# Attention copies pinned in program order, layer 3's stages in forward order, and one layer-3 block less ahead of the second attention table

## The chip, the cores and the metric

The kernel runs on one core of one Trainium2 chip. The metric is the device time of one execution in microseconds (us). A profiled execution also has a span, from its first to its last instruction; all times of day in this document ("at 2089.8 us") count from the start of that span. The engines are TensorE (PE: matrix products; its weight loads are listed apart as PEld), VectorE (DVE), ScalarE (ACT), GpSimd (POOL) and SyncE (SP, which here only issues DMAs).

## The reference

x has 128 graphs of 64 nodes with 256 features, all in float32; adj is one 64x64 matrix. Four layers follow one another, each as `x = layernorm(x + layer(x))`. The change lies in the last two:

```
# layer 2: attention along 512 edges (src, dst), 4 heads of 64
Xq, Xv = H @ W_lin.T, H @ W_val.T
e    = a . leaky_relu(Xq[:, src] + Xq[:, dst], 0.2) + log(A0[src, dst] + 1e-8)
attn = softmax of e over the edges with one src
Y    = sum over those edges of attn * Xv[:, dst];   return Y @ W_out.T

# layer 3: a filter in the eigenbasis U of adj's normalized Laplacian
agg = U.T applied to the nodes of x
h   = relu(agg @ W1 + b1)
return U applied to the nodes of (h @ W2 + b2)
```

Layer 0 (two graph convolutions and four small LSTMs) and layer 1 (a graph convolution with two batch norms) come first and take most of the time; the change does not touch them.

## The kernel before, in words

X stays on the chip as 64 tiles of 128x256 (two graphs each). Layer 2 works on **pairs** of tiles, numbered 0 to 31, in two **halves** of 16 pairs. Layer 3 works on **blocks** of four tiles, numbered 0 to 15.

*Scoring* (`scores`, from L1914) makes the edge scores of a pair. `maps` (L1901) multiplies the transposed X by both weight matrices (L1907); ACT copies the results out as xq (L1909) and xv (L1910), and SP stores xv in DRAM. PE then expands xq to edges (l, L1930), ACT copies l to xs (L1937), DVE applies the leaky relu (L1938), and PE reduces to scores (sc, L1884).

*Softmax* (`softmax`, from L1952) normalizes the scores of one half and scatters the weights to DRAM by eight indirect DMAs that POOL issues (L2002). `fetch(half)` (L2007) reads them back as **table** M2, eight DMAs of 512 KB, four issued by SP and four by POOL (L2012). Table one is the first half's, table two the second half's.

*Values* (`values`, L2040) has one step for each pair k. `load(k+1)` copies eight columns of the table on ACT (mc, L2019, two buffers) and has POOL load that pair's xv from DRAM (xr, L2022, three buffers). `mixed(k)` multiplies the two on PE (L2034, sixteen 64x64 products into two PSUM tiles, of which there are two), and ACT copies each to yT (L2037). PE multiplies the yT of the pair before by W_out (the output product, L2055). `Norm.add` (L1228) adds that to X on DVE (L1234) and takes statistics (L1237, L1238). After four tiles `Norm.flush` (L1243) computes the scale in a chain of small instructions (is_t L1212 on DVE, is_s L1214 on ACT, is_r L1215 to L1217, ln_rs L1218 and ln_sh L1249 on DVE), and ACT normalizes the four tiles (L1253).

*Layer 3* has four stages for a block q. `basis(q)` (L2115) applies U to X on PE (L2120), ACT copies the result (ag, L2122), and POOL adds a constant row to the four tiles of X (L2124). `first_map(q)` (L2126) multiplies by W1 (L2130), and DVE adds the bias and cuts at zero (h, L2133). `back(q)` (L2135) applies U again (L2138), copied by ACT (uh, L2140). `second_map(q)` (L2142) multiplies by W2 (L2148), adds to X on DVE and normalizes as above, and SP writes the tiles out (L2154). `blocks` (L2156) is a generator: its step q runs second_map(q-3), back(q-2), first_map(q-1) and basis(q).

Each of these parts is a generator, and `run(...)` names the order in which their next steps are emitted: this is the **program order**. A scheduler then orders the instructions of each engine by its own planned times and may move an instruction ahead of others on its engine. `tc.keep_in_program_order` takes that freedom from an instruction. On the chip each engine runs its list strictly in order and waits on semaphores.

The order around the change is: scoring steps beside softmax steps of half 0; `fetch(0)`; scoring beside the first seven value steps; then softmax of half 1 beside value steps, with the first layer-3 blocks; `fetch(1)`; a few value steps and blocks; eight turns of two value steps and one block; two value steps; and the remaining blocks.

Of the kernel before, what the change touches and what calls it, by code (L numbers as in the profile page):

```python
# [1259 lines left out]
def tile_adj_resnorm(ctx: ExitStack, tc: tile.TileContext, I: dict, out: bass.AP, layers: int = 4):  # L1260
    nc = tc.nc
    v, s, te = nc.vector, nc.scalar, nc.tensor
# [3 lines left out]
    def load(name, shape, src, eng=nc.sync, dtype=F32):  # L1266
        t = const.tile(shape, dtype, tag=name, name=name)
        eng.dma_start(t, src)
        return t
# [17 lines left out]
    xt = I["x"].rearrange("(t b) n d -> (b n) t d", b=2)  # L1287
    nc.sync.dma_start(X[:, :4, :], xt[:, :4, :])
    ident = load("ident", [P, P], I["ident"], s)
    adj = load("adj", [N, N], I["adj"], s)  # L1290
    wg1 = lh.tile([P, 2, D], F32, tag="wg1", name="wg1")
    nc.sync.dma_start(wg1, kio(I["Wg1"]))
# [4 lines left out]
    s.dma_start(bl, I["bih"])  # L1297
    s.dma_start(bh, I["bhh"])
    cst = load("cst", [N, CONST_COLS], I["consts"], nc.gpsimd)

    ones = const.tile([P, P], F32, tag="ones", name="ones")
# [182 lines left out]
    with tc.tile_pool(name="lw", bufs=1) as lw, tc.tile_pool(  # L1484
# [141 lines left out]
        def residual(g, H, pool, tag):  # L1626
            hj = H.rearrange("p c (m j) -> p c j m", j=TG)
            for j in range(0, TG, 2):
                ps = pool.tile([P, 512], F32, tag=tag, name=tag)
                for i in range(2):  # L1630
                    for c in range(2):
                        te.transpose(ps[:, i * D + c * P : i * D + (c + 1) * P], hj[:, c, j + i, :], ident)
                ln.add(g * TG + j, ps, 2)
                yield
# [21 lines left out]
        with tc.tile_pool(name="l0g", bufs=1) as l0:  # L1656
            back = iter(())
            for g in range(NT // TG):
# [18 lines left out]
                if g < NT // TG - 1:  # L1677
                    back = residual(g, last, pr, "pr")
# [58 lines left out]
    back = residual(NT // TG - 1, H, pp, "ps")  # L1737
# [23 lines left out]
    for q in range(NQ):  # L1761
        h = sm.tile([P, 4, 512], F32, tag="h", name="h")
# [70 lines left out]
    with ExitStack() as l2:  # L1833
# [27 lines left out]
        sc, M2 = [None, None], [None, None]  # L1861
# [145 lines left out]
        def fetch(half):  # L2007

            M2[half] = lw.tile([P, N, P], F32, tag="M2", name="M2")
            for n0 in range(0, N, 16):  # L2010
                for b in range(2):
                    (nc.sync, nc.gpsimd)[b].dma_start(  # L2012
                        M2[half][b * N : (b + 1) * N, n0 : n0 + 16, :],
                        attn_d[b][: N * N, :].rearrange("(d n) q -> d n q", n=N)[:, n0 : n0 + 16, :])

        def load(k):
            half, u_ = divmod(k, HU)
            m = sm.tile([P, 2, 2, 2, N], F32, tag="mc", name="mc")
            s.copy(m.rearrange("p c i h n -> p (c i h) n"),  # L2019
                   M2[half][:, :, u_ * 8 : u_ * 8 + 8].rearrange("p n q -> p q n"))  # L2020
            x = sm.tile([P, 2, D], F32, tag="xr", name="xr", bufs=3)
            nc.gpsimd.dma_start(x, xvd[k])  # L2022
            return m, x
# [16 lines left out]
        def values():  # L2040

            K = NT // 2
            now, yT = load(0), None
            for k in range(K + 1):
                y = yT
                if k < K:
                    m, x = now
                    if k < K - 1:
                        now = load(k + 1)
                    yT = mixed(m, x)  # L2050
                if k:
                    po = scratch()
                    for i in range(2):
                        for c in range(2):
                            te.matmul(po[:, i * D : (i + 1) * D], y[:, i, c, :], wo[:, c, :], start=(c == 0), stop=(c == 1))  # L2055
                    ln.add(2 * (k - 1), po, 2)
                yield

        def run(*steps):
            for x in steps:  # L2060
                next(x, None)
# [11 lines left out]
        val = values()  # L2073
# [34 lines left out]
        with tc.tile_pool(name="l3s", bufs=2) as s3, tc.tile_pool(name="l3p", bufs=6, space=PSUM) as p3:  # L2108
            bank = lambda: p3.tile([P, 512], F32, tag="ps", name="ps")
            ln3 = Norm(nc, s3, X, 4, act=True)  # L2110
            ov = out.rearrange("(t b) n d -> (b n) t d", b=2)
            four = lambda a: a.rearrange("p (j n) -> p j n", j=4)
            ag, h, uh = {}, {}, {}

            def basis(q):  # L2115
                ag[q] = s3.tile([P, 2, 512], F32, tag="ag", name="ag")
                for k in range(2):
                    ps = bank()
                    for j in range(4):
                        te.matmul(ps[:, j * P : (j + 1) * P], X[:, q * 4 + j, k * P : (k + 1) * P], bdu,  # L2120
                                  start=True, stop=True)
                    s.copy(ag[q][:, k, :], ps)  # L2122
                for j in range(4):
                    nc.gpsimd.tensor_tensor(X[:, q * 4 + j, :], X[:, q * 4 + j, :], cb, ALU.add)  # L2124

            def first_map(q):  # L2126
                ps, a = bank(), ag.pop(q)
                for j in range(4):
                    for k in range(2):
                        te.matmul(ps[:, j * P : (j + 1) * P], a[:, k, j * P : (j + 1) * P], w1[:, k, :],  # L2130
                                  start=(k == 0), stop=(k == 1))
                h[q] = s3.tile([P, 4, P], F32, tag="h3", name="h3")
                v.tensor_tensor(h[q], four(ps), nb1[:, None, :].to_broadcast([P, 4, P]), ALU.max)  # L2133

            def back(q):  # L2135
                ps, a = bank(), h.pop(q)
                for j in range(4):
                    te.matmul(ps[:, j * P : (j + 1) * P], a[:, j, :], bdut, start=True, stop=True)  # L2138
                uh[q] = s3.tile([P, 4, P], F32, tag="uh", name="uh")
                s.copy(uh[q], four(ps))  # L2140

            def second_map(q):  # L2142
                a = uh.pop(q)
                n = 4 if q < NT // 4 - 1 else 2
                for j in range(0, 4, 2):
                    ps = bank()
                    for i in range(2):
                        te.matmul(ps[:, i * D : (i + 1) * D], a[:, j + i, :], w2, start=True, stop=True)  # L2148
                    ln3.add(q * 4 + j, ps, 2)
                    t = q * 4 + j + 2  # L2150
                    if t % n == 0:
                        if n == 2:
                            ln3.flush()
                        nc.sync.dma_start(ov[:, t - n : t, :], X[:, t - n : t, :])  # L2154

            def blocks():  # L2156

                NQ = NT // 4
                for q in range(NQ + 3):
                    for k, stage in ((3, second_map), (2, back), (1, first_map), (0, basis)):  # L2160
                        if 0 <= q - k < NQ:
                            stage(q - k)
                    yield

            l3 = blocks()
            sf = soft[1]
            run(sf, val, sf, val, sf, val, sf, val, sf, l3, l3, val, l3, val)
            fetch(1)
            run(l3, val, l3, val, l3)
            run(*[val, val, l3] * 8, val, val, *[l3] * (NT // 4))  # L2170
        valuing.close()

# [61 lines left out]
```

## Time and profile before

| | us |
|---|---|
| median of three runs (2421.91 to 2425.59) | 2422.01 |
| the profiled execution | 2417.21 |
| its span | 2415.4 |
| PE busy in the span | 2292.2 (95%) |
| DVE busy | 1798.8 (74%) |
| ACT busy | 969.7 (40%) |
| POOL busy | 86.3 (4%) |
| span from 2113 to 2192 (scoring beside values): PE busy | 75.60 of 79.00 |
| span from 2196 to 2269 (around table two): PE busy | 65.23 of 73.00 |
| one later turn (2326.88 to 2340.86): PE busy | 12.24 of 13.98 |
| the same turn: DVE, ACT, POOL busy | 8.78, 8.90, 3.83 |
| end (2382.16 to 2415.40): PE, DVE busy | 22.16, 24.40 of 33.24 |

A row of a timeline holds the start in us, the duration in us, the engine, the line of the kernel, the operation, what it writes and reads, and how many instructions were merged; in brackets stands the time that the engine was idle ahead of it and the instruction that released it. A float32 product is two passes on PE, so sixteen products of the program are 32 in the trace. In the list of waits the three numbers are the total in us, the number of waits and the longest. The clock row and the "PEclk" figures give the clock that was granted to PE as a share of its full speed.

### The profile page before, as it was taken

The numbers are of one execution on the slowest core, as the hardware profiler recorded it, in microseconds if no ns is written. First come the engines' busy times: TensorE is split into PE (matmuls) and PEld (weight loads), VectorE is DVE, ScalarE is ACT, GpSimd is POOL, SyncE is SP. The second block draws the span as 40 slices with busy tenths as digits, with TensorE's granted clock in tenths as the row PEclk, the third lists the DMA queues.
The fourth block names the chain that finished last, engine by engine and source line by source line (L and its number), as shares of the span: only waits on it lengthen the run. The fifth ranks groups of instructions, "written<-read, shape, count | busy, mean of one in ns | idle before, by whom it ended". The sixth has DMA issues, their size and how long they took to land. (4 is left out here: it accounts for less than half of the span.)

```text
span 2415.4 us, 29678 instructions
## 1 busy us (share of the span) xinstructions
PE 2292.2 (95%) x9084; PEld 1233.0 (51%) x9084; DVE 1798.8 (74%) x8355; ACT 969.7 (40%) x1751; POOL 86.3 (4%) x131
## 2 busy tenths in 40 slices
PE   7999999999999999999999999998979999899887
PEld 5544654444565544665444644554434433346776
DVE  4666766677887888888888898787958876456656
ACT  2323322242333243332343322334438865456565
POOL 0000000000000000000000000000000000103321
PEclk9999999999999999999999999999989999899999
DMA  6000000000100010100001000012210100311521
GB/s 217 20 18 36 1 35 1 25 28 18 53 1 35 3 51 18 53 35 1 35 36 45 8 18 18 18 51 96 79 36 27 40 30 27 97 39 47 138 80 66
DMA packets 44645, 101.52 MB, mean 42 GB/s; under 512 B 5280, under 2 KB 23840, under 8 KB 43200
## 3 DMA queue, kind: packets, MB, share of 16 engines
q1 hardware_dynamic: 38640, 84.90, 10.1%
q0 software_dynamic: 3984, 14.40, 2.1%
q8 instruction: 72, 1.18, 0.2%
q14 instruction: 93, 0.76, 0.1%
q10 hardware_dynamic: 1856, 0.28, 0.1%
HBM read 67.97 MB, written 31.59 MB: 41 GB/s over the span
## 5 line engine op out<-in xcount | busy, mean ns | idle before, releaser
L1595 PE MATMUL pq<-H,wi 128*128 128x512 f32 (+1 forms) x2016 | 835.0, 546 | 6.1 <-DVE H L1624 4.0
L1601 ACT ACTIVATE gate<-pq,bl 128x512 f32<-128x512 f32 (+1 forms) x504 | 317.2, 634 | 790.0 <-PE pq L1599 645.6
L1595 PEld LDWEIGHTS pq<-H,wi 128*128 128x128 f32 x2016 | 371.7, 190 | 330.6 <-issue 255.4
L1599 PE MATMUL pq<-lh,wh 128*128 128x512 f32 (+1 forms) x1152 | 482.7, 535 | 16.2 <-DVE lh L1619 12.9
L1599 PEld LDWEIGHTS pq<-lh,wh 128*128 128x128 f32 x1152 | 212.8, 190 | 213.2 <-issue 128.3
L1938 DVE SCALAR_TENSOR_TENSOR xs<-xs 128x512 f32<-128x512 f32 x256 | 165.5, 682 | 65.9 <-ACT xs L1937 64.9
L1937 ACT COPY xs<-l 128x512 f32<-128x512 f32 x256 | 136.5, 586 | 74.6 <-PE l L1930 42.2
L1617 ACT ACTIVATE gate<-lc 128x512 f32<-128x512 f32 (+1 forms) x144 | 83.5, 580 | 166.2 <-DVE lc L1613 79.9
L1930 PE MATMUL l<-edge_s,xq 64*128 64x512 f32 x512 | 134.7, 623 | 7.5 <-ACT xs L1937 3.9
L1907 PE MATMUL m<-wqv,xT 128*128 128x512 f32 x256 | 121.9, 614 | 0.8 <-DVE xT L1898 0.8
L1769 PE MATMUL ps<-h,w 128*128 128x512 f32 x256 | 113.4, 602 | 6.9 <-ACT h L1764 6.9
L1750 PE MATMUL ps<-at,w 128*128 128x512 f32 x256 | 115.0, 600 | 3.8 <-ACT at L1746 3.2
L1253 ACT ACTIVATE X<-X,ln_sh,ln_rs 128x256 f32<-128x256 f32 x192 | 99.5, 590 | 34.2 <-DVE ln_sh L1249 33.8
L1237 DVE BATCH_NORM_STATS2 ln_st<-X 128x6 f32<-128x256 f32 x256 | 98.4, 416 | 2.3
L142 DVE COPY AQR<-eps 64x192 f32<-64x192 f32 (+1 forms) x125 | 35.0, 280 | 81.3 <-PE eps L148 81.1
L2022 POOL DMA_DIRECT2D xr<-xv x32 | 17.5, 548 | 2051.0 <-ACT y L1784 1889.5
L1907 PEld LDWEIGHTS m<-wqv,xT 128*128 128x128 f32 x256 | 46.0, 192 | 75.1 <-issue 59.2
L1769 PEld LDWEIGHTS ps<-h,w 128*128 128x128 f32 x256 | 48.6, 192 | 66.5 <-issue 56.5
L1234 DVE TENSOR_TENSOR X<-ps,X 128x512 f32<-128x512 f32 x66 | 44.6, 675 | 46.4 <-PE ps L2055 44.1
L1615 DVE TENSOR_TENSOR gate<-gate 128x512 f32<-128x512 f32 (+1 forms) x72 | 43.4, 604 | 46.0 <-ACT gate L1601 45.5
L1750 PEld LDWEIGHTS ps<-at,w 128*128 128x128 f32 x256 | 46.6, 189 | 58.7 <-issue 46.1
L1930 PEld LDWEIGHTS l<-edge_s,xq 64*128 64x128 f32 x512 | 46.3, 188 | 58.0 <-issue 32.1
(573 smaller groups left out, 3281.9 us busy)
## 6 DMA issues: line engine op xcount, KB each, us to landing
wi<-in_WihT_dram SPq DMA_DIRECT2D x16, 1024.0 KB, 4.9
wh<-in_WhhT_dram SPq DMA_DIRECT2D x12, 1024.0 KB, 6.9
X<-in_x_dram SPq DMA_DIRECT2D x16, 512.0 KB, 8.9
xd<-X SPq DMA_DIRECT2D x16, 512.0 KB, 2.7
X<-xd SPq DMA_DIRECT2D x16, 512.0 KB, 3.4
xv<-xv SPq DMA_DIRECT2D x32, 256.0 KB, 2.0
xr<-xv POOLq DMA_DIRECT2D x32, 256.0 KB, 2.9
out_dram<-X SPq DMA_DIRECT2D x15, 512.0 KB, 2.9
```

What stands on the lines that cost most here:

```text
L1237: nc.vector.bn_stats(st, self.X[:, k, :])
L1253: nc.scalar.activation(x, x, AF.Identity, bias=sh[:, k : k + 1], scale=rs[:, k : k + 1])
L1595: te.matmul(ps, wi[:, kk, o * P : (o + 1) * P], at(kk, k), start=(kk == 0), stop=(k == 0 and kk == 1))
L1599: te.matmul(ps, wh[:, kk, o * P : (o + 1) * P], hst[:, kk, :M], start=False, stop=(kk == 1))
L1601: s.activation(gates[gt][:, c, :M], ps, AF.Tanh if gt == 2 else AF.Sigmoid, bias=bl[:, p - 1, o : o + 1])
L1617: s.activation(g[2], cs, AF.Tanh)
L1750: te.matmul(ps, w1[:, k, c * P : (c + 1) * P], at[:, k, :], start=(k == 0), stop=(k == 1))
L1769: te.matmul(ps, w2[:, k, c * P : (c + 1) * P], h[:, k, :], start=(k == 0), stop=(k == 3))
L1907: te.matmul(ps, xT[:, i, c, :], wqv[:, c, :], start=(c == 0), stop=(c == 1))
L1930: mms.append(te.matmul(pl[i][:, b, :], xq[i][r, c * P : (c + 1) * P], GG[r, :], start=True, stop=True))
L1937: taken.append(s.copy(x, pl[i][:, b, :]))
L1938: ready.append(v.scalar_tensor_tensor(x, x, 0.2, x, ALU.mult, ALU.max))
```

## The change

Three edits, all in the last two layers.

1. In `load`, the copy mc of the first two pairs of each half (u_ below 2: pairs 0, 1, 16 and 17) is kept in program order.
2. A step of `blocks` runs its stages as basis(q), first_map(q-1), back(q-2), second_map(q-3), the reverse of the order before.
3. Ahead of the eight turns, `run` emits two blocks after `fetch(1)` instead of three; the block left out is emitted at the end.

```diff
         def load(k):
             half, u_ = divmod(k, HU)
             m = sm.tile([P, 2, 2, 2, N], F32, tag="mc", name="mc")
-            s.copy(m.rearrange("p c i h n -> p (c i h) n"),
-                   M2[half][:, :, u_ * 8 : u_ * 8 + 8].rearrange("p n q -> p q n"))
+            c = s.copy(m.rearrange("p c i h n -> p (c i h) n"),
+                       M2[half][:, :, u_ * 8 : u_ * 8 + 8].rearrange("p n q -> p q n"))
+            if u_ < 2:
+                tc.keep_in_program_order(c)
...
                 for q in range(NQ + 3):
-                    for k, stage in ((3, second_map), (2, back), (1, first_map), (0, basis)):
+                    for k, stage in enumerate((basis, first_map, back, second_map)):
                         if 0 <= q - k < NQ:
                             stage(q - k)
                     yield
...
             run(sf, val, sf, val, sf, val, sf, val, sf, l3, l3, val, l3, val)
             fetch(1)
-            run(l3, val, l3, val, l3)
+            run(l3, val, l3, val)
             run(*[val, val, l3] * 8, val, val, *[l3] * (NT // 4))
```

No arithmetic changes, and no instruction is added or left out. Behind the edit the lines of the kernel move by two (L2034 becomes L2036, and so on from `load` down).

## The prediction

> **What bounds the kernel now.** The page comes first: TensorE (PE) is busy almost everywhere and dips only in the last sixth.
>
> ```profile
> PE   7999999999999999999999999998979999899887
> PEclk9999999999999999999999999999989999899999
> ```
>
> The change touches nothing before 2076 us, so the rest is read from 1900 us on: first the waits there.
>
> ```profile
> ACT mc L2019 <- DMA M<-attn_d: 13.5, 1, 13.5
> PE m L1896 <- ACT xv L1910: 10.4, 1, 10.4
> PE m L2034 <- ACT yT L2037: 17.7, 10, 3.5
> ```
>
> Three stalls carry the argument. ScalarE (ACT) waits 13.5 us for the first attention table, and PE sits 10.4 us behind it. Then PE waits ten times for yT. The timelines of ACT (two lines) and PE at the first stall:
>
> ```profile
> 2075.25 1.07 ACT L1937 COPY xs<-l 128x512 f32<-128x512 f32 x2 [0.75 <-PE sc L1884]
> 2089.78 2.01 ACT L2019 COPY mc<-M 128x512 f32<-128x512 f32 x2 [13.46 <-DMA M<-attn_d]
> ...
> 2079.99 1.98 PE L1907 MATMUL m<-wqv,xT 128*128 128x512 f32 x4
> 2092.38 1.12 PE L1896 MATMUL m<-ident,X 128*128 128x128 f32 x4 [10.41 <-ACT xv L1910]
> 2094.60 3.79 PE L1930 MATMUL l<-edge_s,xq 64*128 64x512 f32 x8 [1.10 <-ACT xq L1909]
> 2098.32 1.35 PE L1884 MATMUL sc<-xs,az 128*32 128x512 f32 x8
> ```
>
> L1930 x8 takes 3.79 us after the gap and 1.99 us elsewhere: PE comes back at half clock. One turn of the later loop (two value steps, one layer-3 block) lasts 13.97 us, of which PE works 12.23. PE first, then ACT, VectorE (DVE) and GpSimd (POOL):
>
> ```profile
> 2289.56 0.98 PE L2034 MATMUL m<-mc,xr 64*64 64x64 f32 x32
> 2290.47 1.99 PE L2055 MATMUL ps<-wo,yT 128*128 128x256 f32 x8
> 2292.39 0.68 PE L2034 MATMUL m<-mc,xr 64*64 64x64 f32 x16
> 2294.81 0.68 PE L2034 MATMUL m<-mc,xr 64*64 64x64 f32 x16 [1.74 <-ACT yT L2037]
> ...
> 2290.40 1.04 ACT L2122 COPY ag<-ps 128x512 f32<-128x512 f32 x2
> 2291.35 0.37 ACT L2037 COPY yT<-m 128x256 f32<-128x256 f32 x1
> 2292.43 2.08 ACT L1253 ACTIVATE X<-X,ln_sh,ln_rs 128x256 f32<-128x256 f32 x4 [0.71 <-DVE ln_sh L1249]
> 2294.41 0.35 ACT L2037 COPY yT<-m 128x256 f32<-128x256 f32 x1
> ...
> 2290.74 0.49 DVE L1216 TENSOR_TENSOR is_r<-is_r,is_t 128x4 f32<-128x4 f32 x1
> 2291.27 0.65 DVE L1217 SCALAR_TENSOR_TENSOR is_r<-is_r,is_s 128x4 f32<-128x4 f32 x1
> ...
> 2289.12 2.78 POOL L2124 TENSOR_TENSOR X<-X,cb 128x256 f32<-128x256 f32 x4 [6.75 <-PE ps L2120]
> ```
>
> The second yT copy of a value step stands on ACT behind four normalizations (L1253), and the next value product needs the PSUM tile that this copy frees. So PE waits 1.74 us in each turn.
>
> **Part 1: the pinned copies.** The built order shows only ACT moved here: the copies for pairs 0 and 1 now follow sixteen score copies (L1937) and four map pairs and stand just ahead of the first yT. Without the wait, PE goes on at the spacing of the pair before (L1907 at 2069.80 to the end of L1884 at 2075.16 is 5.36 us): L1884 ends at 2079.99+5.36 = 2085.35 instead of 2099.60, 14.25 us earlier. The two copies now stand in the running stream: about 1.05 us each, ahead of yT and the next L1937, for which PE waits; with the seams I take back 2.3. Gain 11.9 us (10 to 14.2). The table lands at 2089.8; the score copies ahead of the moved pair end at 2111.5-14.3 = 2097.2, so 7 us of scoring cover it. Without that cover the wait would return one for one.
>
> **Part 2: table two.** Here order and queues change. POOL's adds (L2124, 0.70 us each): eleven now stand before the last scatter instead of eight, so its half of table two starts about 2 us later but ends its issues at the same 2238. More important is xr of pair 15: it now stands behind eight adds, the last four waiting for PE's basis of block 4 (done about 2241.1), and is issued near 2244 instead of 2240.9. SyncE's half waits for the seventh scatter, which ends at 2231.1 in either order, and its output writes only start later. It shares POOL's queue with the table. In the DMA view of 2241.3 to 2242 us its neighbour took
>
> ```profile
> xr<-xv POOLq DMA_DIRECT2D x2, 256.0 KB, 14.0
> ```
>
> where 2.9 us is the median. [...] By the row it lands when the table does, about 2254.8. I take the row: the table's 2 MB are ahead of it in the same queue. Walking the new PE order with the rows' durations (basis 1.79, first map 1.79, back 0.89, second map 1.73, mixing 0.91, output product 1.92), mixing of pair 15 is reached at 2248.3 and then waits some 6.5 us, with one output product more but one second map less ahead of pair 16. Before loses 3.55+1.82 us there to the table and 2.1 to half clock; after loses 6.5 and, restarting slow, about 2. Both arrive at the end of the sixteenth output product near 2269: 0 (from -5 if xr lands early to +3). Behind that product on PE stand two output products and block 5. The pinned copies of pairs 16 and 17 now stand on ACT behind an ag copy and four normalizations; the table is there by then, so they add their 2 us where PE is waiting anyway or at most 0.5 to it.
>
> **Part 3: the loop.** With the stages from first to last, a block's back copy (L2140) and both yT copies follow one another on ACT, and the layer-3 normalizations come after the second yT. The mixing then finds its PSUM free about 1 us ahead. What is late next? PE's 12.23 us, closely followed by the chain ACT-DVE: ag 1.04, is_s to the first normalization 2.12 (2290.31 to 2292.43), h and sum of the next tile with statistics 0.69+3.5, is_s 0.2, chain with the value sum between 2.3, four normalizations 2.05: 11.9. Seven turns (one fewer than before) each save 1.74: -12.2; the last yT wait (2.34) goes too; +0.8 for one new wait in the first turn; PE also holds one block less, 6.2. The half clock at 2311 to 2315 (0.63, no long gap ahead of it) I leave as it is. From 2269.0 to the last output product: 113.2-12.2-2.3+0.8-6.2 = 93.3 us.
>
> [...] The rows: L1216 and L1217 take 0.49 and 0.65 beside POOL's adds, 0.16 away from them, each ending with an add (2291.21, 2291.90). By the row each chain pays 0.8 us, already in the 2.12 above. [...] I take the row: adds and chain stay beside one another as they are now.
>
> **Part 4: the tail.** Six blocks remain instead of five, and the reversed order leaves second maps last. PE runs 18.6 us of three full steps, then 8.8 more. But DVE needs about 4.8 us a block for sums, statistics and chain (2405.97 to 2410.77 for the last), and after the twelfth block's second map four blocks queue on it. With h, and the last two-row chain behind six normalizations, I get 43.7 us from the last output product to the end, against 33.1 (2382.3 to 2415.4): +10.6, of which 6.2 is the moved block. Bounds +6.2 (DVE hidden as before) to +13.
>
> **Sum**, on the profiled span of 2415.4: -11.9 +0 -19.9 +10.6 = -21.2, span 2394.2. Its execution took 2417.2 us; the median of the three runs is 2422.0, and the difference is put on that: 2400.8.
>
> **Rivals.** (A) the above, 2400.8, seven in ten; its own range 2391 to 2409. (B) The loop keeps its 13.97 us because the chain (11.9, only 0.3 short of PE) takes the place of the yT wait: 12.2 back, 2413; for it the thin margin, against it that the chain's rows already hold the contention. 0.15. (C) xr lands before PE reaches pair 15, by the fit: 5 less, 2396; 0.09. (D) Slower: POOL's adds, now at the head of a block, hold both normalization chains of a turn. [...] It decides from 21.2/14 = 1.5 us a chain; L1216 did once take 2.95 us (2234.2), but in none of the steady turns. 0.06. That the pin does nothing is excluded by the built order.
>
> A measurement of this kernel can tell about 0.2% (4.8 us) from no change. Faster: A, B, C, 0.94; within 0.2% the edge of D, 0.01; slower 0.05. Range 2390 to 2413: A with table two, tail and loop at their bounds one at a time, and B.
>
> **What would show it.** No ACT wait for M near 2080 and no PE gap there; a PE wait for DMA xr of 5 to 7 us before pair 15; turns of 12.2 to 12.5 us without yT waits; a tail of 43 us with DVE nearly full. Wrong if turns stay near 14, or if DVE's L1216 grows past 1 us in them.

## The result, and the profile after

| | us |
|---|---|
| before, median of four runs (2421.28 to 2425.59) | 2421.96 |
| after, median of four runs (2392.08 to 2401.38) | 2397.22 |
| ratio after to before, with its 95% interval | 0.9894 (0.9872 to 0.9916) |
| the profiled execution of after (its span) | 2401.38 (2399.6) |

The change is 25 us faster (20 to 31 by the interval), 3.6 us below the forecast. The profiled execution is the longest of its four, and part of it lies ahead of the change: TensorE reaches L1896 of the same pair at 2080.01 instead of 2071.62. These 8.4 us were gathered in layers 0 and 1, before 1811 us, where nothing was changed: by the clock records of the two traces (the times at which the granted clock changed) PE had spent 51.2 us at half clock up to there instead of 34.1, and half of that difference is 8.5 us. So the two traces are compared stretch by stretch, and the whole difference from L1896 to the end is -24.2 us. The end of a product is taken where PE's next instruction starts.

| stretch of PE's list | before | after | difference | forecast |
|---|---|---|---|---|
| L1896 (2071.62) to the last l product L1930 (2188.58) | 116.96 | 107.95 | -9.0 | -11.9 |
| from there to the end of the sixteenth output product | 80.42 | 75.20 | -5.2 | 0 |
| from there to the end of the last output product | 113.16 | 95.22 | -17.9 | -19.9 |
| from there to the end | 33.24 | 41.22 | +8.0 | +10.6 |
| sum | 343.78 | 319.59 | -24.2 | -21.2 |

The list of PE's waits of after, from 2060 us on (total, number, longest):

```profile
PE m L2036 <- DMA xr<-xv: 8.2, 1, 8.2
PE l L1930 <- ACT xs L1937: 3.1, 7, 1.1
...
PE ps L2150 <- ACT uh L2142: 1.1, 1, 1.1
```

The wait for ACT's xv (10.4 us) is gone, and of the ten waits for yT (17.7) one of 0.2 is left. One wait of 8.2 us for a load of xr is new. Table one in the timelines of after, ACT and then PE:

```profile
2104.66 1.07 ACT L1937 COPY xs<-l 128x512 f32<-128x512 f32 x2 [0.75 <-PE sc L1884]
2105.62 2.07 ACT L2019 COPY mc<-M 128x512 f32<-128x512 f32 x2
...
2105.79 1.12 PE L1930 MATMUL l<-edge_s,xq 64*128 64x512 f32 x2 [1.14 <-ACT xs L1937]
2106.84 0.97 PE L2036 MATMUL m<-mc,xr 64*64 64x64 f32 x32
2107.75 3.54 PE L1930 MATMUL l<-edge_s,xq 64*128 64x512 f32 x6
2111.22 1.93 PE L1884 MATMUL sc<-xs,az 128*32 128x512 f32 x8
```

The pinned copies now start without a wait. But right behind the first mixing product PE runs at half clock for 6.8 us: L1884 takes 1.93 us for what takes 1.06 elsewhere, and the granted clock is 0.53 from 2107.8 to 2115.0 and 1.00 on both sides. The longest gap just ahead of it is the 1.14 us in the rows. One later turn of after, PE, from the block's first product to the next block's:

```profile
2288.36 1.95 PE L2122 MATMUL ps<-bda,X 128*128 128x128 f32 x16
...
2294.64 0.97 PE L2036 MATMUL m<-mc,xr 64*64 64x64 f32 x32
2295.55 1.99 PE L2057 MATMUL ps<-wo,yT 128*128 128x256 f32 x8
2297.47 0.97 PE L2036 MATMUL m<-mc,xr 64*64 64x64 f32 x32
2298.38 1.99 PE L2057 MATMUL ps<-wo,yT 128*128 128x256 f32 x8
...
2300.21 1.95 PE L2122 MATMUL ps<-bda,X 128*128 128x128 f32 x16
```

A turn takes 11.85 us and PE works in all of it. Table two in after, POOL first, then SyncE's queue and PE:

```profile
2233.25 0.98 POOL L2002 DMA_INDIRECT attn_d<-at,edge_s  x1 [0.17 <-issue]
2240.82 2.15 POOL L2012 DMA_DIRECT2D M<-attn_d  x4 [5.82 <-DMA attn_d<-at,edge_s]
2242.96 5.53 POOL L2126 TENSOR_TENSOR X<-X,cb 128x256 f32<-128x256 f32 x8
2248.44 1.65 POOL L2024 DMA_DIRECT2D xr<-xv  x3
...
2232.37 2.38 SPq L2012 DMA_DIRECT2D M<-attn_d  x4
...
2256.12 1.62 PE L2036 MATMUL m<-mc,xr 64*64 64x64 f32 x32 [8.23 <-DMA xr<-xv]
2257.67 5.66 PE L2057 MATMUL ps<-wo,yT 128*128 128x256 f32 x16
```

The eighth scatter is issued at 2233.25 and has landed only at 2240.8. POOL waits for it ahead of its half of the table, and xr(15) stands behind that half and eight adds.

### The profile page after: what moved, and what is told of

Read it like the earlier page. It is cut to its first block, busy times and chain, and to the rows that moved or that the text cites. A ratio compares the mean times of both kernels' runs of the same rounds, so it can differ in the third digit from the quotient of the medians.

```text
span 2399.6 us, 29664 instructions
## 1 busy us (share of the span) xinstructions
PE 2295.5 (96%) x9084; PEld 1230.2 (51%) x9084; DVE 1801.9 (75%) x8355; ACT 972.0 (41%) x1751; POOL 86.8 (4%) x131
## 5 line engine op out<-in xcount | busy, mean ns | idle before, releaser
L1930 PE MATMUL l<-edge_s,xq 64*128 64x512 f32 x512 | 135.5, 621 | 7.3 <-ACT xs L1937 4.8
L142 DVE COPY AQR<-eps 64x192 f32<-64x192 f32 (+1 forms) x125 | 35.1, 280 | 81.2 <-PE eps L148 81.0
L2024 POOL DMA_DIRECT2D xr<-xv x32 | 17.5, 548 | 2065.7 <-ACT y L1784 1898.5
L1930 PEld LDWEIGHTS l<-edge_s,xq 64*128 64x128 f32 x512 | 46.3, 186 | 58.4 <-issue 32.1
L1624 DVE TENSOR_TENSOR H<-gate 128x512 f32<-128x512 f32 (+1 forms) x72 | 46.8, 650 | 33.4 <-ACT gate L1617 27.6
```

The lines of the kernel that those rows point to most:

```text
L1930: mms.append(te.matmul(pl[i][:, b, :], xq[i][r, c * P : (c + 1) * P], GG[r, :], start=True, stop=True))
```

## The experiments

Ratios are to the kernel before, on the same chip, with 95% intervals.

### The edits one by one

Edit 1 alone: the `load` part of the diff on the kernel before.

> Only edit 1 (the pinned copies) on the kernel before. Theory: the 10.4 us PE wait at table one goes and nothing later takes it back; from the trace of after, whose offset of +8.4 us was there before the change begins, the stretch from 2071 to 2187 is 9.0 us shorter, so about 9 us less than before, 2413 (with the forecast's 11.9: 2410); turns of the later loop stay at 13.97 us. Rival: the waits for table two absorb the gain because that table comes no earlier: 2421, no change.

Measured: 2408.0 us, ratio 0.9953 (0.9939 to 0.9966). The stretch from L1896 to the last l product takes 104.66 us, 12.3 less than before. The execution that was profiled is the fastest of the five (2399.6 us), so its stretches show more than the median gained. PE at the first mixing:

```profile
2098.28 1.12 PE L1930 MATMUL l<-edge_s,xq 64*128 64x512 f32 x2 [1.14 <-ACT xs L1937]
2099.33 0.98 PE L2036 MATMUL m<-mc,xr 64*64 64x64 f32 x32
2100.24 1.98 PE L1930 MATMUL l<-edge_s,xq 64*128 64x512 f32 x6
2102.15 1.07 PE L1884 MATMUL sc<-xs,az 128*32 128x512 f32 x8
```

The order and the wait of 1.14 are the same as in after, but here the clock stays full (1.00 from 2090 to 2120): L1930 x6 takes 1.98 us, not 3.54. The rival fell. In this trace the pinned copies also helped at table two: from the last l product to the end of the sixteenth output product it takes 74.1 us instead of 80.4.

Edit 2 alone, the stage order.

> Only edit 2 (stages from first to last), still three blocks. Theory: the stage order alone makes the turn: 11.85 us instead of 13.97, eight turns, 17 us; the tail gives back about 2, the table-two stretch up to 5: 10 to 15 us less than before, 2407 to 2412. The order of GpSimd's list around the scatters is the one of after, so an xr wait of some 8 us should show here too. Rival: the short turn needs the block fewer as well: 2422.

Measured: 2403.1 us, 0.9927 (0.9914 to 0.9941), 18 us less than before. Turns take 11.85 us, so the order of the stages alone makes the short turn. The tail with five blocks takes 35.1 us against 33.2. The expected xr wait did not come: PE waits 5.2 us there ahead of a second map instead, for DVE to free its bank. Behind that wait stands the stall of table one, now at table two. ACT, DVE and PE:

```profile
2262.89 1.05 ACT L2019 COPY mc<-M 128x512 f32<-128x512 f32 x1 [9.81 <-issue]
...
2264.08 0.18 DVE L1215 RECIPROCAL is_r<-is_s 128x4 f32<-128x4 f32 x1 [9.37 <-ACT is_s L1214]
...
2265.11 2.07 PE L2148 MATMUL ps<-w,uh 128*128 128x256 f32 x4 [5.23 <-DVE X L1234]
```

The view of M puts the 9.81 us down to the table: the first copy from table two is not pinned in this kernel and stands on ACT ahead of the is_s that DVE's chain needs.

Edit 3 alone, one block fewer.

> Only edit 3 (one block fewer ahead of the turns). Theory: turns stay at 13.97 us with their yT waits; one block of 6.2 us PE work moves from ahead of the sixteenth output product to the tail: within 3 us of before, 2419 to 2425. Rival: the block fewer is what lets the turn shorten or table two start early: 2405 to 2410.

Measured: 2422.7 us, 1.0004 (0.9995 to 1.0014): nothing. Turns stay at 13.97 us, PE waits 6.6 us for xr, the tail takes 40.7 us. The xr wait comes here although the eighth scatter is early (POOL waits 1.6 us for it at most, and 5.8 in after): with one block less PE has 6.2 us less to do ahead of pair 15.

Edits 2 and 3 without the pin.

> The changed kernel without edit 1 (edits 2 and 3 together). Theory: the gains add: 9 us above the changed kernel, 2406 (by the forecast's 11.9: 2409), with the table-one stall of ScalarE back at 13 us and turns of 11.85 us. Rival: a later wait takes the pin's gain back, so it is worth little: 2397 to 2399.

Measured: 2405.7 us, 0.9939 (0.9925 to 0.9952). That is 11 us behind the changed kernel by the ratios, so the pin is worth in it what it is worth alone (11 us). The xr wait is 9.1 us, and ACT's unpinned copy again waits 10.2 us for table two.

Edits 1 and 2 without edit 3 (the line is again `run(l3, val, l3, val, l3)`).

> Edits 1 and 2 without edit 3: three blocks ahead of the turns, stages forward, copies pinned. Theory: the edits add, so 11.4 and 17.7 us less than before (the ratios of the two kernels with one edit): 2393, 4 us below the changed kernel, with a PE wait of 2 to 5 us at table two and a tail of 35 us. Rival: with the pinned copies the third block is stuck behind the copies that wait for table two on ScalarE, and the block fewer was needed: 2397 to 2402.

Measured: 2391.4 us, 0.9875 (0.9857 to 0.9892). The changed kernel was run once more:

> The changed kernel once more, beside the three others of this call: 2397, as before. If edit 3 costs nothing it stands level with the kernel with edits 1 and 2 (2391); by the tails (41 us against 35, PE work of a block 6.2) the difference lies only around table two and should be within 5 us.

It took 2397.5 us, 0.9896 (0.9881 to 0.9911). Its tail is 41.2 us and its xr wait 8.9. The third edit probably costs 4 to 6 us; the intervals overlap, but the traces name the place. With three blocks PE has 6.2 us more work ahead of pair 15 and waits 3.27 us for xr there instead of 8.2 to 8.9.

### The wait for xr

The adds of the first blocks are emitted behind `fetch(1)` and pinned, so that all scatters stand ahead of them:

```diff
-                for j in range(4):
-                    nc.gpsimd.tensor_tensor(X[:, q * 4 + j, :], X[:, q * 4 + j, :], cb, ALU.add)
+                if late is None:
+                    plus(q)
+                else:
+                    late.append(q)
...
             fetch(1)
+            for q in late:
+                plus(q, True)
+            late = None
```

> The changed kernel, with GpSimd's adds of the first blocks emitted behind fetch(1) and pinned there, so that the eight scatters and GpSimd's half of table two stand ahead of all adds. Theory: the xr wait of 8.2 us comes from the eighth scatter, which is issued at 2233.3, just behind SyncE's half of the table (2232.4 to 2234.1), lands 6.6 us later and so holds GpSimd's half until 2240.8. With the scatters ahead, both halves are issued some 4 and 10 us earlier, xr(15) is there in time, and the wait with its cold restart goes: 8.2 + 2.6 = about 11 us less than the changed kernel, 2386. Rival 1: the 4 MB of the table and the output writes fill the DMA engines anyway: 0 to 3 us, 2394 to 2397. Rival 2: the late adds hold the second map of block 0, which needs them: no gain or a loss, 2397 to 2402.

Measured: 2394.8 us, 0.9880 (0.9861 to 0.9899). The xr wait is gone, as the theory had it: POOL issues its half of the table at 2227.8 instead of 2240.8. But the kernel gains only 2.4 us by the medians and 3.4 by the ratios, not 11, and the intervals overlap. The timelines of POOL, DVE and PE in this kernel:

```profile
2230.00 10.97 POOL L2132 TENSOR_TENSOR X<-X,cb 128x256 f32<-128x256 f32 x16
...
2231.02 9.98 DVE L1212 TENSOR_SCALAR is_t<-ln_mv 128x4 f32<-128x4 f32 x1
...
2242.91 1.50 PE L2122 MATMUL ps<-bda,X 128*128 128x128 f32 x8 [3.74 <-DVE h L2143]
```

A DVE instruction on four numbers a partition, 0.17 us at the median, takes 9.98 us: it starts one microsecond into a run of sixteen adds on POOL (2230.00 to 2240.97) and ends at 2241.00, with them. All that stands behind it on DVE waits, and PE waits 3.7 us for h. This is not the rival as written (no second map waited for its adds' result), but its direction was right.

The same with three blocks:

> Edits 1 and 2, three blocks, and GpSimd's adds of the first blocks behind fetch(1) as in e5. Theory: the table lands some 8 us earlier, so no wait is left between the softmax and the turns: the work is the same as in e5 and the time too, 2386, or up to 3 below it. Rival 1: 2393, as e7, if the adds' place does nothing with three blocks. Rival 2: the late adds hold second maps: 2397 and more.

Measured: 2393.0 us, 0.9878 (0.9861 to 0.9896), level with three blocks alone. The same DVE instruction takes 10.00 us, and PE waits 3.76; right behind, L2140 takes 3.78 us for what takes 1.95 elsewhere (granted clock 0.93 from 2240 to 2280).

Is it POOL's run that holds DVE? In the next kernel the late adds differ from the last one in their engine: DVE adds blocks 0 to 2, and these adds are no longer pinned.

```diff
-                    c = nc.gpsimd.tensor_tensor(X[:, q * 4 + j, :], X[:, q * 4 + j, :], cb, ALU.add)
-                    if pin:
-                        tc.keep_in_program_order(c)
+                    (v if pin else nc.gpsimd).tensor_tensor(X[:, q * 4 + j, :], X[:, q * 4 + j, :], cb, ALU.add)
```

> As the kernel with three blocks and late adds, but the adds of blocks 0 to 2 are done by VectorE instead of GpSimd (twelve instructions, each under 0.5 us by the rows of sums of that size). Theory: nothing holds VectorE any more, its is_t instruction takes 0.2 us instead of 10.0, TensorE's 3.8 us wait goes and no xr wait comes: 2386 to 2389. Rival: VectorE held for another reason (it waits for the eighth scatter or the table): is_t stays long, 2393.

Measured: 2388.6 us, 0.9855 (0.9840 to 0.9870), the lowest median of all kernels here, and below the changed kernel by 9 to 10 us; its interval overlaps those of the kernels with three blocks. DVE in the same chain, and POOL:

```profile
2231.54 0.17 DVE L1212 TENSOR_SCALAR is_t<-ln_mv 128x4 f32<-128x4 f32 x1
2232.53 2.80 DVE L1216 TENSOR_TENSOR is_r<-is_r,is_t 128x4 f32<-128x4 f32 x1
...
2232.51 2.79 POOL L2132 TENSOR_TENSOR X<-X,cb 128x256 f32<-128x256 f32 x4
```

No wait of PE at table two is longer than 0.64 us, and is_t takes 0.75 us at most. Four adds of block 3, which stay on POOL (2232.51 to 2235.30), hold L1216 for 2.80 us, and nothing on PE waits for that. From the last l product to the end the trace takes 201.1 us; with the late adds on POOL it took 209.1. So the theory of the late scatter holds, and so does that of POOL's run.

In the last two, the adds move from basis to back, behind the scatters and behind POOL's half of the table, with three blocks and with two:

```diff
             def back(q):
+                with tc.issue_after(last[0].ins):
+                    for j in range(4):
+                        c = nc.gpsimd.tensor_tensor(X[:, q * 4 + j, :], X[:, q * 4 + j, :], cb, ALU.add)
+                        if q:
+                            tc.keep_in_program_order(c)
```

Here `last[0]` is the last scatter, and from `fetch(1)` on the last load of the table.

> Edits 1 and 2, three blocks; GpSimd's adds of a block moved from basis to back, kept behind the scatters (block 0) and behind its half of table two (the later blocks). Theory: a run of adds on GpSimd holds a small VectorE instruction (16 in a row held one for 10 us); here the runs after the table are 8 and 4, so the hold is 5.5 us at most and TensorE waits under 1 us, with no xr wait: 2386 to 2389. Rival: the hold comes from something else at that place and stays near 10 us: 2393. If the table is not early: 2391, as with edits 1 and 2.

> All three edits, with GpSimd's adds at back as in the kernel beside it. Theory: the xr wait of 8.2 us and its 2.6 us cold restart go: about 2387; level with the three-block version, as the block fewer only moves 6.2 us of TensorE work from ahead of the turns to the tail. Rival: with two blocks TensorE reaches pair 15 before the table even so: 2392 to 2395.

Measured: 2400.8 us, 0.9919 (0.9905 to 0.9932), and 2405.4 us, 0.9940 (0.9927 to 0.9954). Both expectations missed, by 12 us (against 2389) and by 18 (against 2387). The table came early, though with two blocks an xr wait of 3.0 us is left, and the later turns grew. A turn with three blocks, POOL, DVE and PE:

```profile
2306.58 2.78 POOL L2140 TENSOR_TENSOR X<-X,cb 128x256 f32<-128x256 f32 x4
...
2306.29 3.09 DVE L1216 TENSOR_TENSOR is_r<-is_r,is_t 128x4 f32<-128x4 f32 x1
...
2304.73 0.97 PE L2038 MATMUL m<-mc,xr 64*64 64x64 f32 x32 [1.38 <-ACT yT L2041]
...
2318.03 0.98 PE L2038 MATMUL m<-mc,xr 64*64 64x64 f32 x32 [1.37 <-ACT yT L2041]
```

L1216 starts just ahead of the four adds and ends with the last of them (2309.36). A turn takes 13.30 us instead of 11.85, and PE waits for yT again, because one normalization chain is held for 3 us: ACT waits 3.42 us for it at 2310.99, and the next yT copies stand behind (2317.61). In the last turn L1216 is held for 5.82 us beside eight adds, and the turn takes 17.5. This is rival D of the forecast, brought about by another order of POOL's list.

### The tail

The changed kernel, with the stage order of before in the last six steps:

```diff
-                    for k, stage in enumerate((basis, first_map, back, second_map)):
+                    order = ((0, basis), (1, first_map), (2, back), (3, second_map))
+                    for k, stage in order if q < NQ - 3 else order[::-1]:
```

> The changed kernel, with the stages of the last six steps (behind the last value step) in the order of before. By the forecast's tail (43.7 us, of which 33.1+6.2 would be the price of six blocks in the old order) this saves up to 4.4 us: 2393. By the traces of the kernels with one edit (tail 40.6 us with six blocks in the old order, 41.1 in the new; 34.9 against 33.1 with five) it saves 0.5 to 1.8: 2395.5 to 2397.

Measured: 2395.3 us, 0.9884 (0.9863 to 0.9906); not to be told from the changed kernel. The tail in its trace is 40.4 us against 41.2: the order costs about 1 us here, and the rest of the 8.0 is the sixth block.

## Why the prediction was right, and where not

**Part 1** was right in mechanism and size: 14.25 less 2.3 taken back gave 11.9, and the four profiled kernels with the pin whose clock stays full at that place show 12.3 (104.65 or 104.66 against 116.96). The changed kernel's trace shows 9.0, because the half clock behind the first mixing costs 3.3 us. It does so in both profiles of after (107.95 and 107.89), and in four of the experiments. It was not foreseen, and its cause stays open (end of this section).

**Part 2** failed in one step: "its half of table two starts about 2 us later but ends its issues at the same 2238". It ended them at 2243. The forecast counted POOL's own adds and overlooked the transfer that it waits for. In before the eighth scatter is issued at 2231.48 and POOL goes on at 2234.00; in after it is issued at 2233.25, behind the first of SyncE's table loads (2232.37), and lands 6.6 us after its issue ended. The two rows of before:

```profile
2231.48 0.96 POOL L2002 DMA_INDIRECT attn_d<-at,edge_s  x1 [0.40 <-PE ps L2148]
...
2234.00 0.57 POOL L2012 DMA_DIRECT2D M<-attn_d  x1 [0.80 <-DMA attn_d<-at,edge_s]
```

The other traces sort in the same way. In the tail kernel and in the one with three blocks the scatter is issued 0.9 us behind the start of SyncE's loads and lands 6.75 us after its issue ended; with edit 2 alone and with edits 2 and 3 POOL waits 5.9 us for it (5.8 in after). In before it is issued 1.0 us ahead of those loads and lands after 1.6; with the pin alone and with edit 3 alone POOL waits 1.5 and 1.6 us for a scatter at most. So xr(15), expected near 2244, was issued at 2248.4, and PE waited 8.2 us instead of 6.5. The row (xr behind the table lands late) was the right choice: xr(15) took 7.7 us (2248.4 to 2256.1). No run shows the fit that rival C names, on which the -5 in the sum of part 2 (xr landing early) rested; in its place stand these 7.7 us, and PE's waits for xr of 3.0 to 9.1 us in six other profiles.

The measured -5.2 where 0 was forecast is not better than forecast: the block left out lies ahead of the sixteenth output product in the trace, and its 6.2 us were booked behind it. With the block in its place the forecast was -6.2 for part 2 and -13.7 for part 3; measured are -5.2 and -17.9.

**Part 3** was right in mechanism: the yT waits went and nothing took their place, so rival B fell. The mis-sized terms: six turns save 2.12 us each (forecast seven of 1.74), for a turn is 11.85, not 12.23 to 12.5. PE's own work was taken too long: a mixing cut in two by the wait shows 0.68 twice, and 0.97 in one run, and that 0.39 goes with the wait. The last turn saves 2.6 (2.34), the first 0.9, where a new wait of 0.8 was forecast, and the half clock at 2311 (1.7) is not in the trace of after. The chain of 11.9 did not show as a bound: PE waits for nothing in a turn of 11.85, and DVE works 9.59 us of it.

**Part 4** was too dear: 8.0, not 10.6. The failed step is "DVE nearly full" behind the last output product. It works 30.84 us of 41.22. PE waits only once in it, 1.1 us. What is left is the block and the order: by the kernels with one edit the order costs 1.8 us with five blocks (35.1 against 33.2) and 0.5 with six (41.2 against 40.7), and the block the rest, 6.2 to 7.5.

**The total** came within 3 us partly by luck. With the block in its place the four parts missed by +2.9, +1.0, -4.2 and -2.6 us, and these misses offset one another.

**Rival D** did not come in the changed kernel, where a turn takes 11.85 us. There the row of the forecast (0.49 and 0.65) held:

```profile
2291.30 0.61 DVE L1216 TENSOR_TENSOR is_r<-is_r,is_t 128x4 f32<-128x4 f32 x1
2291.94 0.65 DVE L1217 SCALAR_TENSOR_TENSOR is_r<-is_r,is_s 128x4 f32<-128x4 f32 x1
```

Each waits for the end of one add, 0.65 us at most. Longer holds are in other runs: 9.98 us beside sixteen adds, 5.82 beside eight, 3.09 beside four. What one costs a turn, the kernel with three blocks and the adds at back shows: with one chain held for 3.09 us the turn took 13.30, and the other chain of that turn was not held (L1216 0.16 at 2314.36). When DVE gets in after one add, and when only after the run, these runs don't settle: beside the four adds of after at 2289.79, which follow a wait of 2.35 us for PE, the hold was 0.65 at most; beside the four of the kernel with the adds at back at 2306.58 it was 3.09, and beside the eight of that kernel at 2223.60 again 0.65 at most. No kernel separates these cases.

What stays open is why PE's clock falls behind the first mixing in six profiles with the pin and not in the other four, since order and waits there are the same. In the clock records of before and after the half-clock stretches last 3.4 to 17.1 us, this one 6.8. No run separates the six from the four, so the cause is not shown.

## What to carry to other kernels

When instructions change places ahead of a DMA that others wait for, time not only the issue but the landing, and ask which large transfers now start ahead of it: a scatter issued 1.8 us later landed 6.8 us later here. Small element-wise work on GpSimd was not free here, although GpSimd was busy for 4% of the span: sixteen adds held a VectorE instruction of 0.17 us for 9.98, four held one for 3.09. So keep it in short pieces where no chain runs, or give it to VectorE (twelve adds moved there brought the lowest median here). Test each edit alone: of these three, two brought all the gain, and the third probably took some of it back.

## What the runs showed of the hardware

- A VectorE instruction on four numbers a partition, 0.16 to 0.17 us at the median, took 9.98 and 10.00 us beside sixteen GpSimd adds (late adds, two and three blocks). In the kernel with three blocks and the adds at back it took 3.09 beside four in two turns, 5.82 beside eight in the last turn, and 0.65 at most beside eight others (2223.60). Beside the four adds of a turn of the changed kernel it took 0.61.
- A scatter issued 0.9 us behind the start of another queue's 2 MB table loads took 6.6 to 6.8 us from the end of its issue to landing in three profiles (changed kernel, tail, three blocks); issued 1.0 us ahead of them, in before, it took 1.6.
- PE ran at half clock for 6.8 us in after, behind a gap of 1.14 us; behind the same gap with the pin alone the clock stayed at 1.00. The stretch around it took 107.95 us and 104.66.
- Two executions differed by 8.4 us at the same instruction, ahead of any change; PE had run 51.2 us at half clock up to there in one and 34.1 in the other.
